# Where a two-layer attention kernel sums its softmax rows and runs its convolution: row sums of DMAs added on VectorE, the convolution's steps ended one tile earlier, reciprocals and position halves asked for later

## The chip, the cores and the metric

The kernel runs on one core of a Trainium2 chip. The metric is the device time of one execution in microseconds (us), lower is better. The engines of the core are TensorE (PE; its weight loads are listed as PEld), VectorE (DVE), ScalarE (ACT), GpSimd (POOL) and SyncE (SP, which here only issues DMAs). Each has its own queue of instructions; they meet through semaphores.

## The reference

Input x has the shape 2 x 256 x 64 x 64, float32. Two residual layers follow each other, each on a group-normalised x:

```python
x = x + _L0_conv_ref(_gn(x), qkv_w, qkv_b, 8)
x = x + _L1_conv_ref(_gn(x), ...)
```

Layer 0 is softmax attention with 8 heads of 32 channels over all 64 x 64 = 4096 pixels:

```python
attn_logits = jnp.einsum('bhci,bhcj->bhij', q, k) * scale
attn_weights = jax.nn.softmax(attn_logits, axis=-1)
out = jnp.einsum('bhij,bhcj->bhci', attn_weights, v)
```

Layer 1 adds two branches. In one, q, k, v (1x1 convolutions, with a position term made from pixel coordinates) go through attention among 64 pixels that lie 8 apart, and then, after more 1x1 convolutions, through attention within 8 x 8 blocks. In the other, a 1x1 mix of q, k and v over heads goes into a grouped 3 x 3 convolution. The kernel folds the latter's weights into one 3 x 3 convolution of the normalised x, 256 to 256 channels.

## The kernel before

**Stages.** The two images (batches b = 0, 1) are worked one after the other. Each goes through: loading x in 8 tiles `xts[t]` of 8 image rows (512 pixels) and its statistics; normalising and the projections q, k, v of layer 0; attention of layer 0 (`attention0`); layer 1's first attention (`layer1_first`); and its second one with the convolution (`layer1_second`, 8 tiles t). The `x` tiles stay in place: each stage adds its result into them. The x of batch 1 is loaded into the places of batch 0's x tiles when these come free. `Stats` (L256 to L271) makes the mean and 1/deviation, with two small matmuls `pm_l` (L261) and `pv_l` (L269) in between; batch 1's first projection matmul is `p_wk` (L333).

**attention0.** A group g is one head h = g // 2 and one half p = g % 2 of the queries (2048 of them, in four units u of 512). There are 16 groups, each with 32 steps j over 128 keys. For each step and unit, PE makes scores (L426: one 128 x 512 matmul), ScalarE the exponentials (L432), and PE multiplies them by v into `av` (L442, `quarters`: four column quarters of 32, one per unit, in the same PSUM bank). Scores lie in three PSUM tiles `sa`, `sb`, `sc` of 3, 2 and 2 banks. The exponentials go into a ring of 28 units, 7 steps; by their place in it the profile calls them `es` or `v`. Their order on PE, ScalarE and VectorE is the order in which the code is written; a scheduler orders the other queues, POOL and SP among them.

**Row sums.** The softmax denominators need the exponentials summed over all keys. VectorE sums most steps into `added` (the profile calls it `e`; two tiles of 128 x 2 x 512; L471 to L479). The steps listed in `SUMMED` (L380, seven of them) are instead summed by DMAs that POOL issues into four accumulators `acc` of 128 x 512 (L481 to L489; they lie in `es`, in `v` and, two of them, in one tile `pair`; the first of the seven copies, the rest accumulate). What is left is the sum over the 128 partitions: `sum_rows` (L502) multiplies `acc` and `added` by a matrix of ones, into the third bank of an `sa` tile. It is asked for at step 1 of the next group (`wanted`), and PE does it between two steps. `waiting` only asserts the order: the first copy into `acc` may come only after `sum_rows` of the group before.

**finish(g)** (L509) takes each group on: `rows` copied by ScalarE (L515), sent through DRAM to spread it over the partitions (`dense`), at step 8 reduced and inverted by VectorE (L521 to L523), sent back as `drec` and broadcast by four DMAs into `avs` (L524 to L526); at step 13 VectorE multiplies the group's `av` by it (L530) and SP writes the result to `ctx` (L532). The last group (15) goes through `finish_last` instead, without DMAs. `add_output` brings the results back and adds them into x, in two steps each, planned by `in_two` (L582 to L591).

**Position halves.** For layer 1, coordinates and their weights are split into a rounded part and the rest: `split` (L148) copies on ScalarE (L152) and subtracts on VectorE (L153). `stack` and `stack_positions` call it and then issue SP DMAs. These run in groups 1 to 5 of batch 0, in two calls: a beginning at step 3 or 15 and a rest at step 12 or 24, by the list `later`.

**layer1_second.** Per tile t: the branch q (two 1x1 convolutions, `phq`, `prq`), a convolution step, the branch k (`phk`, `prk`), scores `sp` (L890), softmax on VectorE and ScalarE, a convolution step, transposes `at` (L910), copies into `bd` (L919), values `pvs` (L873), the product `pc` (L928), and ScalarE's `res` (L939). Convolution has 16 steps per batch: 4 strips s of two tiles by 4 column terms q. Each has a transform on POOL (L785 to L802, one step ahead), 32 matmuls into `mm` (L811), one ScalarE copy and VectorE passes that add it into x tiles 2s and 2s+1 (L817 to L838). Tile 0 runs three steps, tiles 1 to 6 two, tile 7 one. When both x tiles of a strip have their four terms, VectorE adds `res` and x (L1132) and SP writes the output (L1135). `group_attention` takes `apart=True`: the first half of the values comes before the scores, the second after the `bd` copies, and both are copied by ScalarE.

Of the kernel before, what the change touches and what calls it, by code (L numbers as in the profile page):

```python
# [17 lines left out]
P = 128  # L18
# [22 lines left out]
def direct_layers(ctx: ExitStack, tc: tile.TileContext, a: dict, out: bass.AP, bad: bass.AP):  # L41
# [79 lines left out]
    def load_layer1():  # L121
        for name in ("fq2", "fk2"):
            wts[name] = load_const("wt_" + name, [P, KC, C], a[name].rearrange("(k p) m -> p k m", p=P))
        wts["b3"] = load_const("b3", [P, KC], a["b3"].rearrange("(k p) -> p k", p=P))
        wts["rate1"] = load_const("rate1", [P, 1], a["rate1"].partition_broadcast(P))
        wts["rate2"] = load_const("rate2", [P, 1], a["rate2"].partition_broadcast(P))


        posk, posq = w4([4, C], "posk"), w4([4, C], "posq")
        nc.gpsimd.dma_start(out=posk, in_=a["posk"])  # L130
        nc.gpsimd.dma_start(out=posq, in_=a["posq"])
        rows = const.tile([4, 1], F32, name="pos_rows")
        nc.gpsimd.memset(rows, 8.0)
        nc.gpsimd.memset(rows[0:1, :], 1.0)
        nc.vector.tensor_scalar(posq, posq, rows, None, ALU.mult)
        def stack(name, rows):
            wts[name] = const.tile([16, C], F32R, name="st_" + name)
            pair = split(rows, name)
            for g in range(4):
                nc.sync.dma_start(out=wts[name][4 * g : 4 * g + 4].bitcast(F32), in_=pair[:, g % 2, :].bitcast(F32))  # L140

        later.append(lambda: (lambda: stack("posq", posq)))
        later.append(lambda: (lambda: stack("posk", posk)))
# [3 lines left out]

    def split(rows, nm):  # L148

        n, cols = rows.shape  # L150
        pair = w4([n, 2, cols], f"pair_{nm}", F32R)
        nc.scalar.copy(pair[:, 0, :], rows)  # L152
        nc.vector.tensor_sub(pair[:, 1, :], rows, pair[:, 0, :].bitcast(F32))  # L153
        return pair


    kept_w = {name: dram.tile([P, KC, C], F32, name="kept_" + name) for name in ("w3", "fv")}
# [12 lines left out]
    def stack_positions(t):  # L170
        n = slice(t * T, (t + 1) * T)
        loc = w4([4, T], f"loc_{t}")
        nc.sync.dma_start(out=loc, in_=a["loc"][:, n])

        def rest():
            pair = split(loc, f"loc_{t}")
            for d in range(2):
                nc.sync.dma_start(out=loc_kept[:, d, :, n].rearrange("l r n -> r l n"), in_=pair.bitcast(F32))

        return rest  # L180

    def fold_products():

# [193 lines left out]

    RING, RING_A = 28, 17

    SUMMED = (5, 9, 13, 17, 21, 25, 28)  # L380


    SUMMED_LAST = (NJ - 2, NJ - 1)
# [1 line left out]
    def attention0(b, xts, held):  # L385
# [52 lines left out]
        def quarters(dst, lhs, rhs, start, stop, part=None):  # L438

            n = slice(0, T) if part is None else slice(part * T // 2, (part + 1) * T // 2)  # L440
            for u in range(4):
                nc.tensor.matmul(dst[HD0 * u : HD0 * u + HD0, n], lhs, rhs(u)[:, n], start=start, stop=stop)  # L442
# [57 lines left out]
                )  # L500

        def sum_rows(g, rows):  # L502
            waiting.clear()
            quarters(rows, ones, lambda u: acc[u], True, False)
            for j in SUMMED_LAST if g == last else ():
                quarters(rows, ones, lambda u: unit(g, j, u), False, False)
            quarters(rows, ones, lambda u: added[g][u // 2][:, u % 2, :], False, True)

        def finish(g):  # L509

# [68 lines left out]
        def at_block(g, j, what):  # L579
            also.setdefault((g, j), []).append(what)  # L580
# [7 lines left out]
        for w in (2, 3):  # L588
            in_two((last, 4), (last, 18), add_output(1, w, P - HD0))
        for w in (0, 1):  # L590
            in_two((last, 17), (last, 22), add_output(1, w))  # L591
        st = Stats(xts, f"l1_{b}")
        for t in range(NT):
            at_block(last - 2, 3 * t + 6, lambda t=t: st.tile(0, t))
# [5 lines left out]
        rests = {}  # L600
        for n, begin in enumerate(later):
            at_block(1 + n // 2, 3 + 12 * (n % 2), lambda n=n, begin=begin: rests.update({n: begin()}))
            at_block(1 + n // 2, 12 + 12 * (n % 2), lambda n=n: rests.pop(n)())
        later.clear()

# [3 lines left out]
        def steps():  # L609

            for done in range(NH0 * 2 * NJ):
                g, j = divmod(done, NJ)
                for _ in work_of(g, j):
                    yield done
                if g and j == 1:
                    wanted.append(late[0].send)
                    waiting.append(g)
                if g and j in (8, 13):
                    next(late[0])
                for what in also.get((g, j), ()):  # L620
                    what()
                if j == 4 and g % 2 == 0 and g // 2 + 1 < NH0:
                    fetch_head(b, g // 2 + 1, held)
                if j == NJ - 1:
                    avs = w4([P, 2, T], f"avs_{b}_{g}")
                    nc.scalar.copy(avs[:, 0, :], sums[g])
                    copied[g] = avs
                    late[:] = [finish(g)]
                    next(late[0])
                    if g + 2 < NH0 * 2:  # L630
                        fetch_queries(b, g + 2, held)
                yield done + 1
# [411 lines left out]
    def layer1_second(b, xts, feats, mean, rstd, shift, pacc):  # L1044
# [28 lines left out]
        for t in range(NT):  # L1073
            nt = f"sr_{b}_{t}"
            f = [
                feats[k][:, 8 * t : 8 * t + 8].rearrange("p o d e -> p (o d e)") for k in range(KC)
            ]

            def branch(one, two, col1, col2, nm):
                hid = w4([P, KC, T], f"h{nm}_{nt}")  # L1080
                for m in range(KC):
                    ph = bank([P, T], f"ph{nm}_{nt}_{m}")
                    for k in range(KC):
                        nc.tensor.matmul(  # L1084
                            ph, wts[one][:, k, m * P : (m + 1) * P], f[k], start=k == 0, stop=k == KC - 1
                        )
                    bn_relu(hid[:, m, :], ph, col1, m)
                res = w4([P, KC, T], f"r{nm}_{nt}")
                pr = [bank([P, T], f"pr{nm}_{nt}_{m}") for m in range(KC)]
                for k in range(KC):  # L1090
                    for m in range(KC):
                        nc.tensor.matmul(  # L1092
                            pr[m], wts[two][:, k, m * P : (m + 1) * P], hid[:, k, :], start=k == 0, stop=k == KC - 1
                        )
                for m in range(KC):
                    bn_relu(res[:, m, :], pr[m], col2, m)
                return res

            with tc.manual_schedule(engines={mybir.EngineType.PE}):
                q = branch("fq1", "fq2", V_FQ1, V_FQ2, "q")  # L1100
                for tt in {0: (3, 4)}.get(t, (t + 4,)):
                    if tt < NT:
                        to_image(tt)
                if t == 0:
                    wf = fetch_conv_weights(b)
                if t + 1 < NT:
                    conv()
                k = branch("fk1", "fk2", V_FK1, V_FK2, "k")
                res = w4([P, KC, T], f"res_{nt}")

                def to_res(m, pc, res=res):

                    bn_relu(
                        res[:, m, :].rearrange("p (d o e) -> p o d e", d=8, o=8),
                        pc.rearrange("p (o d e) -> p o d e", o=8, d=8), V_SRW, m,
                    )

                parts = group_attention(
                    nt, q, k, lambda c, w, f=f: f[c][:, w * P : (w + 1) * P], wts["fv"], to_res, apart=True
                )  # L1120
                next(parts)
                conv()
                next(parts)
                next(parts, None)
                if t == 0:
                    conv()
            conv_edges(xts, t)
            results[t] = res
            for n in sorted(n for n in results if done >= 4 * (n // 2 + 1)):
                res = results.pop(n)  # L1130
                for m in range(KC):
                    nc.vector.scalar_tensor_tensor(  # L1132
                        res[:, m, :], res[:, m, :], wts["rate1"], xts[n][:, m, :], ALU.mult, ALU.add
                    )
                nc.sync.dma_start(  # L1135
                    out=out[b, :, n * T : (n + 1) * T].rearrange("(k p) n -> p k n", p=P), in_=res
                )


    for b in range(B):  # L1140
# [15 lines left out]
        with tc.tile_pool(name=f"ps1_{b}", bufs=8, space=PSUM) as psum["ps"]:  # L1156
            between = layer1_first(b, xts, check, st)
        with (
            tc.tile_pool(name=f"ps2_{b}", bufs=4, space=PSUM) as psum["ps"],
            tc.tile_pool(name=f"pacc_{b}", bufs=1, space=PSUM) as pacc,  # L1160
        ):
            layer1_second(b, xts, *between, pacc)

# [557 lines left out]
```

## Time and profile before

| | us |
|---|---|
| three runs | 3258.98, 3260.95, 3265.7 (median 3260.95) |
| profiled run, its span | 3260.86, 3259.0 |

Where the time of the profiled execution goes, by stage (windows of the trace; busy us of each engine):

| stage | from to, us | length | PE | DVE | ACT | POOL |
|---|---|---|---|---|---|---|
| attention of layer 0, b = 0 | 108 to 1171 | 1063 | 1048.8 | 912.3 | 976.6 | 286.0 |
| layer 1 first, b = 0 | 1171 to 1350 | 179 | 152.6 | 149.2 | 73.1 | 9.5 |
| layer 1 second, b = 0 | 1350 to 1655 | 305 | 286.9 | 144.3 | 99.5 | 119.1 |
| loading, projection, b = 1 | 1655 to 1743 | 88 | 85.6 | 36.2 | 26.6 | 0.0 |
| attention of layer 0, b = 1 | 1743 to 2798 | 1055 | 1044.6 | 907.2 | 971.9 | 285.9 |
| layer 1 first, b = 1 | 2798 to 2969 | 171 | 146.8 | 62.0 | 59.6 | 0.8 |
| layer 1 second, b = 1 | 2969 to 3259 | 290 | 278.1 | 134.7 | 91.9 | 115.2 |

Read a row so: where an engine's busy time comes close to the length, little can be hidden behind something else there. Two thirds of the span are layer 0's attention. Busy time does not tell which wait ends last; for that the lists of waits and the timelines are needed. In those, a line names the engine, the source line, the operation, and the tiles as out<-in; in brackets stands the time for which the engine had been idle, and who ended it.

### The profile page before, as it was taken

The page shows a single profiled execution, that of the slowest core. Times are in us where ns is not written, and L with a number is a line of the kernel's source. Part 1 is how long each engine was busy: PE and PEld are TensorE (multiplying, and loading weights), DVE is VectorE, ACT ScalarE, POOL GpSimd, SP SyncE. Part 2 cuts the span into 40 slices and gives each one's busy share as a digit, 9 for nine tenths or more (in the row PEclk, how much of TensorE's full clock was granted, in tenths as well). Part 3 has the DMA queues.
Part 4 walks back from the last instruction along what each step waited for, and adds up shares of the span by engine and source line. Part 5 has one row for each costly group of instructions (what it writes and reads, how often), then busy time and mean ns, then how long its engine had stood idle before and what let it go on. Part 6 is the DMA issues. An engine that isn't in the chain of part 4 may idle for free. (4 is left out here: it accounts for less than half of the span.)

```text
span 3259.0 us, 62523 instructions
## 1 busy us (share of the span) xinstructions
PE 3129.8 (96%) x25113; PEld 1845.7 (57%) x25113; DVE 2394.0 (73%) x3122; ACT 2327.3 (71%) x2370; POOL 837.0 (26%) x929
## 2 busy tenths in 40 slices
PE   7999999999999979999989999999999999799998
PEld 4455555555555535676654555555555555356665
DVE  4688878987989898654446888879889798624443
ACT  2798989999999963523326999999999999624232
POOL 2122222222222220343201222322222222104431
PEclk9999999999999989999989999999999999899999
DMA  7967869679795641300149688796797956400000
GB/s 257 255 135 160 160 135 183 134 163 179 146 186 124 137 108 49 137 26 26 43 177 262 132 163 162 148 182 134 159 181 146 179 124 137 122 2 10 14 20 21
DMA packets 243916, 425.23 MB, mean 130 GB/s; under 512 B 99008, under 2 KB 109592, under 8 KB 241184
## 3 DMA queue, kind: packets, MB, share of 16 engines
q0 software_dynamic: 98336, 241.20, 38.3%
q1 hardware_dynamic: 145280, 179.93, 20.7%
q8 instruction: 199, 3.26, 0.4%
q14 instruction: 101, 0.83, 0.1%
HBM read 118.26 MB, written 67.86 MB: 57 GB/s over the span
## 5 line engine op out<-in xcount | busy, mean ns | idle before, releaser
L479 DVE TENSOR_TENSOR e<-e,es 128x1024 f32<-128x1024 f32 (+1 forms) x950 | 1035.4, 1151 | 59.4 <-ACT es L432 58.8
L442 PE MATMUL av<-es,v 128*32 128x256 f32 (+1 forms) x9644 | 746.9, 390 | 0.0
L432 ACT ACTIVATE es<-sa 128x1536 f32<-128x1536 f32 (+1 forms) x444 | 635.9, 1432 | 92.2 <-PE sa L426 46.5
L479 DVE TENSOR_TENSOR e<-e,v 128x1024 f32<-128x1024 f32 (+1 forms) x630 | 669.7, 1120 | 22.1 <-ACT v L432 21.7
L426 PE MATMUL sa<-q,k 128*128 128x512 f32 x1736 | 561.2, 430 | 14.0 <-issue 4.5
L442 PE MATMUL av<-v 128*32 128x256 f32 (+1 forms) x6228 | 506.9, 389 | 0.0
L442 PEld LDWEIGHTS av<-es,v 128*32 128x32 f32 x9644 | 316.5, 109 | 300.1 <-issue 161.3
L426 PEld LDWEIGHTS sa<-q,k 128*128 128x128 f32 x1736 | 280.2, 188 | 297.6 <-issue 139.9
L426 PE MATMUL sc<-q,k 128*128 128x512 f32 x1180 | 373.3, 397 | 10.2 <-ACT es L432 7.5
L426 PE MATMUL sb<-q,k 128*128 128x512 f32 x1180 | 371.4, 396 | 4.4 <-ACT es L432 2.3
L442 PEld LDWEIGHTS av<-v 128*32 128x32 f32 x6228 | 216.3, 109 | 178.4 <-issue 81.4
L432 ACT ACTIVATE es<-sc 128x1024 f32<-128x1024 f32 x296 | 306.4, 1035 | 7.0 <-DVE e L479 7.0
L432 ACT ACTIVATE v<-sc 128x1024 f32<-128x1024 f32 x294 | 304.4, 1035 | 0.9 <-DMA es<-v 0.7
L432 ACT ACTIVATE es<-sb 128x1024 f32<-128x1024 f32 x296 | 302.1, 1021 | 3.6 <-DMA acc<-es 3.6
L432 ACT ACTIVATE v<-sb 128x1024 f32<-128x1024 f32 x294 | 300.1, 1021 | 4.7 <-DVE e L479 3.0
L426 PEld LDWEIGHTS sc<-q,k 128*128 128x128 f32 x1180 | 209.2, 188 | 86.3 <-ACT es L432 20.5
L426 PEld LDWEIGHTS sb<-q,k 128*128 128x128 f32 x1180 | 220.1, 188 | 61.5 <-ACT es L432 4.9
L489 POOL DMA_DIRECT2D es<-es x118 | 101.5, 860 | 526.5 <-ACT es L432 469.8
L432 ACT ACTIVATE v<-sa 128x1536 f32<-128x1536 f32 (+1 forms) x146 | 209.2, 1433 | 34.0 <-PE sa L426 15.1
L811 PE MATMUL mm<-v,wf 128*128 128x256 f32 x1024 | 227.9, 381 | 0.0
L801 POOL TENSOR_TENSOR v<-col 128x512 f32<-128x512 f32 x128 | 161.8, 1294 | 228.5 <-PE sp_sr L890 93.3
L811 PEld LDWEIGHTS mm<-v,wf 128*128 128x128 f32 x1024 | 193.2, 190 | 33.1 <-issue 7.2
(240 smaller groups left out, 3319.4 us busy)
## 6 DMA issues: line engine op xcount, KB each, us to landing
acc<-es POOLq DMA_DIRECT2D x122, 512.0 KB, 6.2
acc<-v POOLq DMA_DIRECT2D x76, 512.0 KB, 6.3
es<-es POOLq DMA_DIRECT2D x136, 256.0 KB, 3.7
v<-es POOLq DMA_DIRECT2D x132, 256.0 KB, 4.6
k<-wk_halves SPq DMA_DIRECT2D x64, 512.0 KB
q<-wq_halves SPq DMA_DIRECT2D x256, 128.0 KB
v<-v POOLq DMA_DIRECT2D x92, 256.0 KB, 4.9
es<-v POOLq DMA_DIRECT2D x88, 256.0 KB, 3.8
```

The source lines that it names most:

```text
L426: nc.tensor.matmul(sc[:, i, :], held["k", g // 2][:, j * P : (j + 1) * P], held["q", g, u // 2][:, u % 2, :], start=True, stop=True,)
L432: nc.scalar.activation(dst, sc[:, i : i + m, :], AF.Exp, scale=SC0)
L442: nc.tensor.matmul(dst[HD0 * u : HD0 * u + HD0, n], lhs, rhs(u)[:, n], start=start, stop=stop)
L479: nc.vector.tensor_add(dst[:, s, :], dst[:, s, :], src)
L489: nc.gpsimd.dma_start(out=dst, in_=src, accum_op=ALU.add)
L801: (nc.gpsimd.tensor_add if plus else nc.gpsimd.tensor_sub)(dst, rows(one), rows(two))
L811: nc.tensor.matmul(mm[:, m, r, :], wf[:, k, 4 * r + q, m * P : (m + 1) * P], v[r // 2][:, r % 2, k, :], start=k == 0, stop=k == KC - 1,)
```

## The change

It has these parts:

1. In groups 0 to 14, `sum_rows` multiplies only `added` by ones. Before it, at step 0 of the next group, VectorE adds the four `acc` into `added` (two adds of 128 x 512 and one of 128 x 1024). `waiting` is moved accordingly. Group 15 is as before.
2. `SUMMED` names other steps, seven again.
3. `finish`'s reciprocal and multiply move from steps 8 and 13 to 9 and 17; `add_output(1, w)` for w = 0, 1 from steps 17 and 22 of the last group to 21 and 26.
4. The position halves are done in three calls instead of two: ScalarE's copy moves from step 12 (24) to step 8 (20), the subtraction and the DMAs stay.
5. Tile 7 of `layer1_second` runs no convolution step, tile 1 runs three. In tile 7 `apart` is false: scores first, then both halves of the values, the second copied by VectorE.
6. The pool of `mm` is opened ahead of the pool of the other PSUM tiles.

```diff
@@ -135,9 +135,16 @@
         nc.vector.tensor_scalar(posq, posq, rows, None, ALU.mult)
         def stack(name, rows):
             wts[name] = const.tile([16, C], F32R, name="st_" + name)
-            pair = split(rows, name)
-            for g in range(4):
-                nc.sync.dma_start(out=wts[name][4 * g : 4 * g + 4].bitcast(F32), in_=pair[:, g % 2, :].bitcast(F32))
+            pair, second = split(rows, name)
+
+            def rest():
+                second()
+                for g in range(4):
+                    nc.sync.dma_start(
+                        out=wts[name][4 * g : 4 * g + 4].bitcast(F32), in_=pair[:, g % 2, :].bitcast(F32)
+                    )
+
+            return rest
 
         later.append(lambda: (lambda: stack("posq", posq)))
         later.append(lambda: (lambda: stack("posk", posk)))
@@ -146,12 +153,12 @@
     later = []
 
     def split(rows, nm):
+
 
         n, cols = rows.shape
         pair = w4([n, 2, cols], f"pair_{nm}", F32R)
         nc.scalar.copy(pair[:, 0, :], rows)
-        nc.vector.tensor_sub(pair[:, 1, :], rows, pair[:, 0, :].bitcast(F32))
-        return pair
+        return pair, lambda: nc.vector.tensor_sub(pair[:, 1, :], rows, pair[:, 0, :].bitcast(F32))
 
 
     kept_w = {name: dram.tile([P, KC, C], F32, name="kept_" + name) for name in ("w3", "fv")}
@@ -172,12 +179,17 @@
         loc = w4([4, T], f"loc_{t}")
         nc.sync.dma_start(out=loc, in_=a["loc"][:, n])
 
-        def rest():
-            pair = split(loc, f"loc_{t}")
-            for d in range(2):
-                nc.sync.dma_start(out=loc_kept[:, d, :, n].rearrange("l r n -> r l n"), in_=pair.bitcast(F32))
-
-        return rest
+        def halves_of():
+            pair, second = split(loc, f"loc_{t}")
+
+            def rest():
+                second()
+                for d in range(2):
+                    nc.sync.dma_start(out=loc_kept[:, d, :, n].rearrange("l r n -> r l n"), in_=pair.bitcast(F32))
+
+            return rest
+
+        return halves_of
 
     def fold_products():
 
@@ -377,7 +389,7 @@
 
     RING, RING_A = 28, 17
 
-    SUMMED = (5, 9, 13, 17, 21, 25, 28)
+    SUMMED = (3, 7, 11, 15, 18, 22, 26)
 
 
     SUMMED_LAST = (NJ - 2, NJ - 1)
@@ -500,11 +512,11 @@
                 )
 
         def sum_rows(g, rows):
-            waiting.clear()
-            quarters(rows, ones, lambda u: acc[u], True, False)
-            for j in SUMMED_LAST if g == last else ():
-                quarters(rows, ones, lambda u: unit(g, j, u), False, False)
-            quarters(rows, ones, lambda u: added[g][u // 2][:, u % 2, :], False, True)
+            if g == last:
+                quarters(rows, ones, lambda u: acc[u], True, False)
+                for j in SUMMED_LAST:
+                    quarters(rows, ones, lambda u: unit(g, j, u), False, False)
+            quarters(rows, ones, lambda u: added[g][u // 2][:, u % 2, :], g < last, True)
 
         def finish(g):
 
@@ -588,7 +600,7 @@
         for w in (2, 3):
             in_two((last, 4), (last, 18), add_output(1, w, P - HD0))
         for w in (0, 1):
-            in_two((last, 17), (last, 22), add_output(1, w))
+            in_two((last, 21), (last, 26), add_output(1, w))
         st = Stats(xts, f"l1_{b}")
         for t in range(NT):
             at_block(last - 2, 3 * t + 6, lambda t=t: st.tile(0, t))
@@ -600,6 +612,7 @@
         rests = {}
         for n, begin in enumerate(later):
             at_block(1 + n // 2, 3 + 12 * (n % 2), lambda n=n, begin=begin: rests.update({n: begin()}))
+            at_block(1 + n // 2, 8 + 12 * (n % 2), lambda n=n: rests.update({n: rests[n]()}))
             at_block(1 + n // 2, 12 + 12 * (n % 2), lambda n=n: rests.pop(n)())
         later.clear()
 
@@ -612,16 +625,23 @@
                 g, j = divmod(done, NJ)
                 for _ in work_of(g, j):
                     yield done
+                if g and j == 0:
+
+                    for w in range(2):
+                        dst = added[g - 1][w]
+                        for s in range(2) if w == 0 else (slice(0, 2),):
+                            nc.vector.tensor_add(dst[:, s, :], dst[:, s, :], acc[s] if w == 0 else pair)
+                    waiting.clear()
                 if g and j == 1:
                     wanted.append(late[0].send)
-                    waiting.append(g)
-                if g and j in (8, 13):
+                if g and j in (9, 17):
                     next(late[0])
                 for what in also.get((g, j), ()):
                     what()
                 if j == 4 and g % 2 == 0 and g // 2 + 1 < NH0:
                     fetch_head(b, g // 2 + 1, held)
                 if j == NJ - 1:
+                    waiting.append(g)
                     avs = w4([P, 2, T], f"avs_{b}_{g}")
                     nc.scalar.copy(avs[:, 0, :], sums[g])
                     copied[g] = avs
@@ -1116,13 +1136,14 @@
                     )
 
                 parts = group_attention(
-                    nt, q, k, lambda c, w, f=f: f[c][:, w * P : (w + 1) * P], wts["fv"], to_res, apart=True
+                    nt, q, k, lambda c, w, f=f: f[c][:, w * P : (w + 1) * P], wts["fv"], to_res, apart=t + 1 < NT
                 )
                 next(parts)
-                conv()
+                if t + 1 < NT:
+                    conv()
                 next(parts)
                 next(parts, None)
-                if t == 0:
+                if t < 2:
                     conv()
             conv_edges(xts, t)
             results[t] = res
@@ -1156,8 +1177,8 @@
         with tc.tile_pool(name=f"ps1_{b}", bufs=8, space=PSUM) as psum["ps"]:
             between = layer1_first(b, xts, check, st)
         with (
+            tc.tile_pool(name=f"pacc_{b}", bufs=1, space=PSUM) as pacc,
             tc.tile_pool(name=f"ps2_{b}", bufs=4, space=PSUM) as psum["ps"],
-            tc.tile_pool(name=f"pacc_{b}", bufs=1, space=PSUM) as pacc,
         ):
             layer1_second(b, xts, *between, pacc)
```

## The prediction

> **What bounds the kernel now.** I read the page's busy table first, then windows by stage, then the waits, and last the timelines of the four places that the edits touch.
>
> ```profile
> PE 3129.8 (96%) x25113; PEld 1845.7 (57%) x25113; DVE 2394.0 (73%) x3122; ACT 2327.3 (71%) x2370; POOL 837.0 (26%) x929
> 200.00:1150.00 950.00, 939.06 (x9139) 527.53 (x9141) 816.26 (x831) 872.79 (x831) 255.85 (x312) 1.00 0.78 155
> 1850.00:2800.00 950.00, 942.70 (x9219) 531.40 (x9215) 822.22 (x832) 875.51 (x828) 258.37 (x315) 1.00 0.78 157
> ```
>
> The busy table covers the span of 3259.0 us. The windows (stretch, length, then busy us of PE, PEld, DVE, ACT, POOL) hold most of layer 0's attention, once per batch. TensorE is busy 939 of 950 us there, and the granted clock is 1.00. The share alone would not prove a bound, so I looked at PE's idle time too: 11 and 7 us, in a few lumps. TensorE bounds both stretches, ScalarE follows at 92%, VectorE at 86%. A group of 32 steps lasts about 66 us. Hence a matmul taken out is worth its duration, and VectorE work put in is free as long as nobody waits for it.
>
> The waits view (engine, tile and line, whom it waited for: us, times, longest) tells who waits for VectorE's inputs:
>
> ```profile
> POOL es L487 <- PE sa L442: 520.0, 30, 19.9
> DVE avs L530 <- DMA avs<-drec: 148.1, 24, 12.4
> DVE e L479 <- ACT es L432: 58.8, 63, 3.8
> ```
>
> VectorE stands still for 148 us at L530 (the row sums' reciprocals, coming back by DMA) and 59 us for fresh exponentials.
>
> **What the Trainium skill says.** (1) "TensorE: Matmul & The Clock Gate", Part 3 (packing small matmuls): matmuls in different column tiles overlap, and matmuls start and end in order. The trace agrees: the quarters below start 0.01 us apart, so four cost what one does. (2) Same page, "Architectural detail": VectorE's queue is strictly first in, first out. The trace agrees: nothing behind L530 starts in its 11.30 us wait. (3) "VectorE: DVE Perf Modes", the tier table: a float32 tensor_tensor has no faster mode than 1x, 2293 ns for 2048 elements; estimate for 1024, half of it: 1.15 us. The trace's adds of 128x1024 take 1.218 us (median), those of 128x512 0.68 us; I use these. (4) "DMA: Bandwidth & Descriptors", rules: an accumulating DMA must not meet another access of the same bytes. That is why `acc` may be written again only after VectorE has read it.
>
> **The change, part by part.**
>
> *Row sums.* The timeline of one group's row sums before:
>
> ```profile
> 526.65 0.59 PE L442 MATMUL sa<-es,ones 128*32 128x512 f32 x1
> 526.66 0.59 PE L442 MATMUL sa<-v,ones 128*32 128x512 f32 x1
> 526.67 0.60 PE L442 MATMUL sa<-acc,ones 128*32 128x512 f32 x2
> 527.08 0.59 PE L442 MATMUL sa<-es,ones 128*32 128x512 f32 x1
> 527.09 0.59 PE L442 MATMUL sa<-v,ones 128*32 128x512 f32 x1
> 527.10 0.60 PE L442 MATMUL sa<-acc,ones 128*32 128x512 f32 x2
> 527.51 1.04 PE L442 MATMUL sa<-e,ones 128*32 128x512 f32 x8
> ```
>
> The matmuls on `acc` (each of the float32 operands makes two passes) fill 526.65 to 527.51, 0.86 us without idle time. They go in 15 of 16 groups, twice: 30 x 0.86 = **25.8 us off PE**, on the path.
>
> VectorE gets 2 x 0.68 + 1.22 = 2.58 us per group, 77 us in all, at step 0 of the next group. Before, it idles 9 to 10 us per group (148.1/30 = 4.9 at L530, (58.8 + 21.7)/30 = 2.7 for exponentials, the rest smaller), so its load goes from about 57 to 59.5 of 65 us. In the 30 groups it finished a group's adds 4.2 to 13.1 us before PE used `added`; less 2.58, PE still finds the sums ready with 1.6 us or more. The last accumulating DMA was issued 14.6 to 19.5 us before the row sums and lands in 6.2 us; its step now comes two earlier, 4 us, while VectorE reads `acc` about 3 to 5 us earlier than PE did, so the new wait (queued behind it: VectorE's adds of steps 1 and on) finds its data. POOL's first copy waits for VectorE's adds instead of PE; it waited 520/30 = 17 us per group before, and the ring place of the exponentials that it reads is needed seven steps later. New waits: 0; they can't gain anything, and I bound them by 0.5 us per group (+15). SUMMED keeps seven steps: 0.
>
> *Reciprocals later, position halves in three.* The timeline (start, us; in brackets the idle time before, and its releaser) shows how a wait of VectorE gets to PE:
>
> ```profile
> 420.83 0.69 DVE L530 TENSOR_TENSOR avs<-avs 128x512 f32<-128x512 f32 x1 [11.30 <-DMA avs<-drec]
> 422.77 1.02 ACT L432 ACTIVATE es<-sc 128x1024 f32<-128x1024 f32 x1 [5.18 <-DVE e L479]
> 423.85 1.22 PE L426 MATMUL sc<-q,k 128*128 128x512 f32 x2 [4.53 <-ACT es L432]
> 285.78 0.73 PE L426 MATMUL sc<-q,k 128*128 128x512 f32 x2 [1.55 <-ACT es L432]
> 2183.27 0.73 PE L426 MATMUL sb<-q,k 128*128 128x512 f32 x2 [1.60 <-ACT v L432]
> ```
>
> The multiply waits, the adds behind it do not free exponentials, ScalarE has no slot, PE no scores. Most of the 148 us never reach PE; these lumps do: 4.53 + 1.55 + 1.60 + 0.2 smaller = 7.9 us. From reciprocal to multiply now lie 8 steps of 2.05 us, 16.4, not 5 (10.2). Where VectorE waited, reciprocal to multiply took 8 to 19 us, in two groups of batch 0 18.7 and 22.8 with the loc_kept transfers ahead in SP's queue. Pushing the multiply back removes most of each wait: over all groups at most 35.8 us of 148 are left. The position halves no longer make VectorE wait for ScalarE's copy (22.2 us in 6 waits at L153). The output steps in the last group come four steps later, still before their use: 0. **-8 us**, between 0 (the lumps return elsewhere) and -9.
>
> *Convolution out of tile 7.* The third step in tile 1 costs there what it saves in tile 7, 6.9 us of matmul: net 0, its transform (POOL, idle 74%) and its one `mm` buffer being ready as they are in tile 0, where the third step starts without a gap. The gain is at the ends. PE at the change of batch before:
>
> ```profile
> 1636.86 2.23 PE L928 MATMUL pc_sr<-bd,vs_sr 128*128 128x128 f32 x16
> 1650.57 0.56 PE L261 MATMUL pm_l<-mv_l,group 128*128 128x2 f32 x2 [11.49 <-DVE mv_l L260]
> 1651.96 0.59 PE L269 MATMUL pv_l<-d_l,group 128*128 128x2 f32 x2 [0.84 <-DVE d_l L266]
> 1655.10 1.22 PE L333 MATMUL p_wk<-xn,wqk 128*128 128x512 f32 x1 [2.54 <-DVE xn L283]
> ```
>
> From 1639.09 to 1655.10 PE idles 16.0 us, all but the two small matmuls. The next batch's last x tile could be loaded only once VectorE had finished the output of tile 6 and 7 (convolution step 16 adds into both): SP issued it at 1644.15, statistics started 1648.64. After, x tiles 6 and 7 get their last convolution term in tile 6, the load of x_7 goes out during tile 7 (27 us long, the load about 4.5), and `pm_l` waits only for the banks that ScalarE reads at the end (0.9 us after `pc`); then the 4.6 us from `pm_l` to `p_wk` stay: about 5.5 us in place of 16.0, **-10.5**. Against it, in tile 7 no convolution matmuls cover the softmax. With scores first and both value halves after them (3.8 us, softmax 2.5 us), PE waits 0.95 us for ScalarE's `rk` and 1.4 us for the `bd` copies that VectorE does behind the value copy (0.69 + 0.42 + 0.43): +2.35. Net **-8.2** (bounds -10.5 and +2.4).
>
> The end of batch 1 has the same +2.35 up to `pc`, but the chain after it shrinks: from `pc` at 3247.86 VectorE ran until 3252.48 through z, edges and four output passes, with two transfers behind it and the end at 3259.0. After, ScalarE's 1.6 us, two output passes of 0.7 us and one transfer follow. I take **-1.5** (between +1 and -3).
>
> *Pool order.* It only moves PSUM banks; no row prices it. 0, within 1 us either way.
>
> Sum on the span: -25.8 - 8 - 8.2 - 1.5 = -43.5; I give 1 back for waits that a faster PE uncovers at ScalarE. 3259.0 - 42.5 = 3216.5. The profiled run took 3260.86, 1.9 above its span; the three runs had 3258.98 to 3265.7, median 3260.95. So **3218 us** in the runs' measure.
>
> **The rivals.**
> B, the lumps do not come back as time: PE idle stays or VectorE's longer list makes new lumps of the same size. For it: VectorE goes to 91%. Only rows, transition and end then count: 3261 - 35.5 = 3225.5, up to 3235 with 0.3 us more per group.
> C, the gap between batches stays (x_7, a pool's release or weights hold `pm_l`): 3218 + 10.5 = 3228.5. Against it: x_7's place is free a tile earlier by the order of instructions.
> D, slower: VectorE becomes the bound. If reading `acc` waits for the last accumulation, or the adds arrive late, PE stands before the row-sum matmuls in every group. It decides from 42.5/30 = 1.4 us stall per group; at 3 us, +90 - 42.5: 3308. Against it: 1.6 us of slack in the worst group, 5 to 10 in most, and idle time of 5 us per group left.
> E, it doesn't do what it says: the tile 1 step stalls PE for a buffer for as long as it saves. Twice 6.9 us: 3232.
>
> **How the numbers follow.** Main case 0.60 (3211 to 3226), B 0.20, C with E 0.09, larger gains than the lumps I counted 0.05 (3205), D 0.06, part of which ends within 0.2%. 0.2%, 6.5 us, is about what a measurement of this kernel can tell from no change. Faster 0.93, same 0.02, slower 0.05. The range, 3208 to 3236, leaves out D and the ends of the others.
>
> **What would show it.** Right: no `acc` matmuls on `ones` but in the last groups; 3 adds more per group and a group near 65 us; L530's wait below 36 us; no PE idle above 1 us within attention but at its start; `p_wk` of batch 1 5 to 6 us after the last `pc`. Wrong: PE waiting for VectorE at `sa<-e,ones`, VectorE waiting for `acc` transfers, `pm_l` still waiting for the statistics, PE gaps before `mm` in tile 1.

## The result and the profile after

The changed kernel takes 3227.03 us (median of four runs, 3224.2 to 3230.66) beside 3260.55 us for the kernel before (four runs, the three of the table above among them); the ratio is 0.9895, 95% interval 0.9878 to 0.9912. That is 33.5 us less, where 42.5 were forecast. The profiled execution has a span of 3227.1 us, 31.9 less than the one before. Line numbers from here on are those of the changed kernel: the exponentials are L444, the adds into `added` L491, the multiply L542, the new adds of `acc` L633.

The busy table, and the windows over layer 0's attention (first score to last score) of both kernels; first the changed kernel:

```profile
PE 3106.4 (96%) x24873; PEld 1843.5 (57%) x24873; DVE 2484.7 (77%) x3230; ACT 2323.5 (72%) x2368; POOL 822.5 (25%) x913
108.98:1152.25 1043.27, 1033.11 (x10036) 586.26 (x10036) 951.88 (x978) 974.25 (x927) 278.40 (x341) 1.00 0.80 161
1720.70:2765.20 1044.50, 1031.68 (x10036) 586.66 (x10036) 945.91 (x964) 970.60 (x917) 278.46 (x341) 1.00 0.80 160
```

then the kernel before:

```profile
108.46:1170.00 1061.54, 1047.83 (x10155) 588.74 (x10156) 910.91 (x925) 975.57 (x927) 285.97 (x349) 1.00 0.78 158
1743.00:2797.60 1054.60, 1044.23 (x10155) 588.28 (x10156) 906.80 (x911) 971.54 (x917) 285.54 (x349) 1.00 0.79 158
```

Attention gave 18.3 and 10.2 us, 28.5 of the 31.9. (In a line of windows stand the stretch, its length, the busy time of PE, PEld, DVE, ACT and POOL, then PE's granted clock, the busy share of the DMA engines and GB/s.) VectorE works some 40 us more in each, and PE is still busy 99% of the time. The timeline of PE at a group's row sums, after:

```profile
256.48 0.61 PE L454 MATMUL av<-v 128*32 128x256 f32 x8
256.92 1.04 PE L454 MATMUL sa<-e,ones 128*32 128x512 f32 x8
257.77 1.05 PE L454 MATMUL av<-v 128*32 128x256 f32 x16
```

The block is 0.86 us long where it was 1.72 (526.65 to 528.37 in the kernel before), and PE does not wait ahead of it. The waits view of the changed kernel:

```profile
DVE e L491 <- ACT es L444: 91.3, 134, 2.5
DVE e L491 <- ACT v L444: 52.0, 64, 3.5
DVE avs L542 <- DMA avs<-drec: 12.5, 7, 2.5
```

The wait at the multiply fell from 148.1 us to 12.5. VectorE now spends its idle time in many short waits for ScalarE, at most 3.5 us long: it is ahead of its work, not behind. The new adds (L633) wait for nothing, and nobody waits for them.

PE's idle time within attention, summed over the trace, group 0 apart from the other fifteen (two batches together):

| | attention, us (b = 0, b = 1) | idle in group 0 | idle in groups 1 to 15 |
|---|---|---|---|
| before | 1061.55, 1054.66 | 5.9 | 18.2 |
| after | 1043.26, 1044.47 | 11.9 | 11.1 |

The idle time that the forecast wanted to win back was won (7.1 us less in groups 1 to 15), but group 0 gave 6.0 of it away. This is one of two places that the forecast had at zero. The timelines of ScalarE, PE and POOL in group 0 of the changed kernel:

```profile
117.57 0.55 POOL L499 DMA_DIRECT2D v<-es  x1
133.24 1.02 ACT L444 ACTIVATE es<-sc 128x1024 f32<-128x1024 f32 x1 [4.01 <-DMA v<-es]
134.31 1.22 PE L438 MATMUL sc<-q,k 128*128 128x512 f32 x2 [3.82 <-ACT es L444]
```

One of the first copies into `acc` is issued at 117.57. The ring place that it reads is still not free at 129, so ScalarE, and PE behind it, stand. It lands only 15.5 us after its issue; the first copies of groups 1 to 15 land in 2.3 to 6.0 us. The windows there show what goes with it, and what else it costs:

```profile
120.00:130.00 10.00, 10.00 (x102) 5.89 (x101) 8.65 (x8) 8.79 (x8) 0.89 (x1) 1.00 1.01 213
130.00:134.30 4.30, 0.49 (x3) 0.06 (x1) 1.86 (x3) 1.02 (x1) 0.86 (x1) 0.77 0.96 216
134.30:150.00 15.70, 15.69 (x138) 8.51 (x139) 10.82 (x10) 12.81 (x12) 4.24 (x5) 0.84 1.17 229
```

The DMA engines are full at the start of attention (share about 1; SP sends keys and queries there). A full share alone makes no lump: in the kernel before it is 1.09 from 400 to 419 us, and PE has no idle time there. And after the lump PE's clock is 0.84, as a mean over 15.7 us, although it is busy all the time.

The second place is the convolution. PE's and VectorE's timeline in tile 2 of batch 0, changed kernel:

```profile
1431.86 0.69 DVE L268 BATCH_NORM_STATS2 stats_l<-x 128x6 f32<-128x512 f32 x1 [4.79 <-DMA x<-in_x_dram]
1432.47 0.67 DVE L837 TENSOR_TENSOR z<-z,mm 128x512 f32<-128x512 f32 x1
1436.35 8.77 PE L831 MATMUL mm<-v,wf 128*128 128x256 f32 x32 [2.47 <-DVE z L840]
```

PE waits 2.47 us before `mm`, for VectorE's passes over the step before (that of the extra step in tile 1). Those were queued behind statistics of batch 1's x, which waited 4.79 us for their load. Batch 1, with no next batch, has no such gap. The six traces with this order of convolution steps (the changed kernel, e1, e5, e6, e8, e9) all have it in batch 0: 2.47 us in three, 3.69 us in e1, e5 and e6.

The change of batch went as forecast:

```profile
1626.18 2.02 PE L948 MATMUL pc_sr<-bd,vs_sr 128*128 128x128 f32 x16 [1.42 <-DVE bd L939]
1629.07 0.38 PE L273 MATMUL pm_l<-mv_l,group 128*128 128x2 f32 x2 [0.87 <-ACT res_sr L959]
1630.63 0.47 PE L281 MATMUL pv_l<-d_l,group 128*128 128x2 f32 x2 [1.18 <-DVE d_l L278]
1633.65 1.22 PE L345 MATMUL p_wk<-xn,wqk 128*128 128x512 f32 x1 [2.54 <-DVE xn L295]
```

`pc` ends at 1628.20, `p_wk` starts 5.45 us later. `pm_l` no longer waits for the statistics but for ScalarE.

### The profile page after: what moved, and what is told of

Its sections match the earlier page's. It is cut to its first block, busy times and chain, and to the rows that moved or that the text cites. A ratio compares the mean times of both kernels' runs of the same rounds, so it can differ in the third digit from the quotient of the medians.

```text
span 3227.1 us, 62236 instructions
## 1 busy us (share of the span) xinstructions
PE 3106.4 (96%) x24873; PEld 1843.5 (57%) x24873; DVE 2484.7 (77%) x3230; ACT 2323.5 (72%) x2368; POOL 822.5 (25%) x913
## 5 line engine op out<-in xcount | busy, mean ns | idle before, releaser
L491 DVE TENSOR_TENSOR e<-e,es 128x1024 f32<-128x1024 f32 (+1 forms) x956 | 1040.6, 1146 | 92.6 <-ACT es L444 91.3
L491 DVE TENSOR_TENSOR e<-e,v 128x1024 f32<-128x1024 f32 (+1 forms) x640 | 676.5, 1111 | 53.2 <-ACT v L444 52.0
L444 ACT ACTIVATE es<-sa 128x1536 f32<-128x1536 f32 (+1 forms) x444 | 635.6, 1432 | 94.6 <-PE sa L438 52.2
L438 PE MATMUL sa<-q,k 128*128 128x512 f32 x1736 | 561.9, 431 | 16.2 <-ACT es L444 5.5
L444 ACT ACTIVATE es<-sc 128x1024 f32<-128x1024 f32 x296 | 306.9, 1037 | 7.1 <-DMA v<-es 7.1
L444 ACT ACTIVATE es<-sb 128x1024 f32<-128x1024 f32 x296 | 302.1, 1020 | 5.0 <-DMA acc<-es 5.0
L444 ACT ACTIVATE v<-sc 128x1024 f32<-128x1024 f32 x294 | 304.9, 1037 | 0.2 <-DMA acc<-v 0.2
L444 ACT ACTIVATE v<-sb 128x1024 f32<-128x1024 f32 x294 | 300.0, 1020 | 0.4 <-DMA acc<-v 0.4
L444 ACT ACTIVATE v<-sa 128x1536 f32<-128x1536 f32 (+1 forms) x146 | 209.2, 1433 | 33.4 <-PE sa L438 13.7
```

Of the source, the lines that this page charges most:

```text
L438: nc.tensor.matmul(sc[:, i, :], held["k", g // 2][:, j * P : (j + 1) * P], held["q", g, u // 2][:, u % 2, :], start=True, stop=True,)
L444: nc.scalar.activation(dst, sc[:, i : i + m, :], AF.Exp, scale=SC0)
L491: nc.vector.tensor_add(dst[:, s, :], dst[:, s, :], src)
```

## The experiments

Theory S: the DMA-summed steps that come earlier, costed at nothing, put group 0's first copies into the full DMA queues. Theory T: the extra step in tile 1 meets the statistics on VectorE's queue. Against them stand L (the lumps were only shifted, or VectorE's longer list makes them), U (in tile 6 the extra step would only move the loss to the change of batch) and, for the whole change, the rivals B and D of the prediction. Each kernel was timed beside the kernel before; its median moved between 3259.6 and 3261.8 us from one set of runs to the next.

**Group 0 later (e1).** From the changed kernel:

```diff
+    SUMMED_FIRST = (5, 9, 13, 17, 20, 23, 26)
+    def summed(g):
+        return SUMMED_FIRST if g == 0 else SUMMED
...
-                if j in SUMMED:
+                if j in summed(g):
...
```

> The changed kernel, but group 0 of each batch keeps DMA-summed steps that begin at 5 (5, 9, 13, 17, 20, 23, 26), all other groups as changed. Theory S (the earlier steps put the first copies into the busy DMA stretch at the start of attention, so ring places come free late): PE's idle time in group 0 falls from 5.2 and 6.7 us to about 2.8 and 3.1 as before the change, 6 us in all; about 3221 us. Rival L (the lumps moved there from the later groups, or VectorE's longer list makes them): group 0 stays at 5 to 7 us, time stays at 3227.

Measured 3221.65 us, ratio 0.9872 (0.9853 to 0.9892). Group 0 idles 2.7 and 2.9 us, attention takes 1039.24 and 1040.54 us: 8.0 less than in the changed kernel, 6.3 of it idle time in group 0. The first copies still take 10.7 to 12.8 us to land, but they go out 3.2 us later after the first score, and their places are needed two steps later. S holds, L falls.

**Only group 0 earlier (e2).** The same function in the kernel before, with (3, 7, 11, 15, 18, 22, 26) for group 0 alone.

> The kernel before, with only group 0's DMA-summed steps at the changed places (3, 7, 11, 15, 18, 22, 26). Theory S: PE's idle time in group 0 rises from 2.8 and 3.1 us to 5 to 7 each, about 6 us slower than before, 3266. Rival L: no change, 3260.

Measured 3269.56 us, ratio 1.0024 (1.0013 to 1.0034): slower by this alone. Group 0 idles 5.7 and 5.5 us. S holds from the other side, without any of VectorE's new adds.

**The extra step in tile 6 (e3).** From the changed kernel:

```diff
-                if t < 2:
+                if t in (0, NT - 2):
                     conv()
```

> The changed kernel with the extra convolution step at the end of tile 6 instead of tile 1. Theory T (the 2.47 us gap before mm in tile 2 of batch 0 comes from VectorE's queue: the statistics of the next batch's x tile wait for its load ahead of the step's passes, and the next step follows too soon): no gap of PE before mm above 0.5 us, and the gap from the last pc to p_wk stays near 5.5 us: 2.5 us less, about 3224.5. Rival U: the passes of the last step run into tile 7, x_7 is loaded later and the gap to p_wk grows by more than 2.5 us: 3227 or more.

Measured 3225.37 us, ratio 0.9886 (0.9868 to 0.9904). The time alone hardly tells it from 3227.0, the trace does: the gap is gone from `mm`, and `p_wk` follows the last `pc` after 5.56 us. PE and VectorE in the same place of this kernel:

```profile
1426.21 7.07 PE L831 MATMUL mm<-v,wf 128*128 128x256 f32 x32
1427.34 1.29 DVE L268 BATCH_NORM_STATS2 stats_l<-x 128x6 f32<-128x512 f32 x2 [4.86 <-DMA x<-in_x_dram]
```

The statistics wait as before, but no unfinished convolution step stands behind them. The same 32 matmuls take 7.07 us where they took 8.77 after the gap, and the stretch between the two attentions is 562.96 us long, not 568.46. That stretch varies: it is 566.2 to 571.9 us long in the six traces with the extra step in tile 1, longest where the gap is 3.69 us, and 563.0 to 566.4 in the four with it in tile 6 (e3, e4, e10, e11), none of which has the gap. The means differ by 4.6 us. T holds, U falls.

**Both repairs (e4).**

> Both edits of the two kernels above together. If S and T hold: 6 + 2.5 us less than the changed kernel, about 3218.5. If L and U hold: 3227 or more.

Measured 3216.04 us, ratio 0.9854 (0.9837 to 0.9872). With the two terms repaired that the forecast had at zero, the time is 2 us from the forecast of 3218. That it comes so close is in part luck, as the last part on the prediction shows: two of its other terms are wrong in opposite directions.

**Row sums on PE again (e5).** From the changed kernel: `sum_rows` and `SUMMED` as before, the adds at step 0 out, the rest of the change kept.

```diff
-            if g == last:
-                quarters(rows, ones, lambda u: acc[u], True, False)
+            waiting.clear()
+            quarters(rows, ones, lambda u: acc[u], True, False)
...
-                            nc.vector.tensor_add(dst[:, s, :], dst[:, s, :], acc[s] if w == 0 else pair)
```

> The changed kernel with the row sums as before it: PE multiplies acc by ones in every group, VectorE adds nothing at step 0, and the DMA-summed steps are the old ones (5 to 28). Sum of my prediction: 25.8 us more PE work, less the 6 us that group 0's earlier steps cost: about 3247. Rival (VectorE's extra 77 us cost PE time by new waits): less than 15 us more than the changed kernel, below 3242.

Measured 3243.2 us, ratio 0.9951 (0.9933 to 0.9969); attention 1050.79 and 1049.37 us. Beside the changed kernel that is 16.2 us more, close to the rival's limit of 15, but the old `SUMMED` also takes away what group 0 had lost. The kernel to compare it with is e1, which begins at the same step in group 0: 20.4 us between the two attentions, 21.5 us between the medians. The row-sum matmuls are worth that, together with what the other steps of `SUMMED` do in groups 1 to 15, which was not tried alone. The block itself is 0.859 us shorter in the trace, in each of 30 groups, 25.8 us in all; some 5 us are lost again. Idle gaps account for 2.1 of them (16.5 us in e1, 14.4 here), and 1.7 are lost in e1 while PE is busy: after a lump of 1.66 us its clock is 0.83, as a mean over 10 us (1756.66 to 1766.66), and in e5 it shows no such drop within attention. The rest, some 1.6 us, was not pinned down.

The kernel before and e5 have the same PE work and steps of DMA sums in attention. Their difference there, 16.0 us, is what the later reciprocals gave, with the position halves and the output steps of the last group, while the row sums were on PE.

**Reciprocals at the old steps (e6).** From the changed kernel:

```diff
-                if g and j in (9, 17):
+                if g and j in (8, 13):
```

> The changed kernel with reciprocal and multiply at steps 8 and 13 again. As predicted for the lumps: VectorE's wait at the multiply rises from 12.5 us to 100 to 150 us and PE's idle time outside group 0 from 11.1 to 18 or more: 3234 or a little above. Rival (the lumps went for another reason, the order of VectorE's adds or the faster steps): PE's idle time outside group 0 stays within 2 us, 3227.

Measured 3240.01 us, ratio 0.9934 (0.9913 to 0.9956): 13 us more for two constants. Its four runs lie between 3232.72 and 3242.53 us, and the traced one is the slowest. The wait at the multiply is back:

```profile
DVE avs L542 <- DMA avs<-drec: 93.3, 17, 9.3
```

PE idles 16.2 us in groups 1 to 15, where the changed kernel has 11.1. The direction and the mechanism are as expected. The wait and the idle time are smaller than expected (100 to 150 us, 18 us or more), the time is longer. Between the two traces the attentions differ by 10.4 us; 3.3 us lie in the stretch between them, which the edit does not touch (the gap before `mm` is 3.69 us here). So some 10 us belong to the two constants, as far as one trace of each can tell. In one of the 30 groups the last new add ends at 1043.99 us here, 0.9 us after PE has begun that group's row sums; in the others the sums are ready 0.4 us or more ahead, where the changed kernel has 6.2 us at least. So without the later multiply VectorE's new adds have no room left in the worst group.

**Convolution as before (e7).** From the changed kernel, the tile loop of the kernel before.

```diff
-  apart=t + 1 < NT
+  apart=True
...
-                if t + 1 < NT:
-                    conv()
+                conv()
...
-                if t < 2:
+                if t == 0:
```

> The changed kernel with the convolution as before: one step in tile 7, two in tile 1, values apart in tile 7. From the parts measured in the trace: the gap to p_wk 16.0 in place of 5.45 us (+10.5), the gap before mm gone (-2.5), tile 7's two waits gone (-1.9 per batch), the end of batch 1 longer (+3.0): about +7, 3234. Rival (the move is worth nothing because what it closes opens elsewhere): 3227.

Measured 3231.2 us, ratio 0.9913 (0.9895 to 0.9932). The gap from `pc` to `p_wk` is 15.76 us again and there is no gap before `mm`. 4 us more than the changed kernel where 7 were expected; at 0.2% that can't be told from 7. The stretch between the attentions is 573.97 us, 5.5 longer than in the changed kernel and 4.8 longer than the mean of the six traces with that order.

**VectorE's new adds twice (e8).** Each add of `acc` is done twice, so `acc` counts twice in these softmax denominators.

```diff
+                            for _ in range(2):
-                            nc.vector.tensor_add(dst[:, s, :], dst[:, s, :], acc[s] if w == 0 else pair)
+                                nc.vector.tensor_add(dst[:, s, :], dst[:, s, :], acc[s] if w == 0 else pair)
```

> The changed kernel with VectorE's three adds of acc done twice in every group 0 to 14, so acc is counted twice in these denominators: 2.58 us more per group, 77 us in all. Theory (VectorE still has room, about 4 us per group): PE's idle time in attention rises by less than 10 us, 3227 to 3237. Rival D (VectorE is at its limit): a part of the 77 us that matters, 3250 to 3300, with PE waiting for VectorE before the row sums.

Measured 3227.4 us, ratio 0.9907 (0.9888 to 0.9925): no difference. VectorE is busy 2555.1 us, 70 more, and PE's idle time in attention is 23.8 us, 0.8 more. The sums are ready 6.2 to 9.5 us before PE uses them in the changed kernel and 2.6 to 6.8 us here. What shrank is VectorE's waits for ScalarE's exponentials, in the waits view of this kernel:

```profile
DVE e L491 <- ACT es L444: 51.8, 84, 2.9
DVE e L491 <- ACT v L444: 26.5, 39, 3.7
```

Rival D falls with room to spare.

**Position halves and pools as before (e9).** Both undone in the changed kernel.

```diff
-            at_block(1 + n // 2, 8 + 12 * (n % 2), lambda n=n: rests.update({n: rests[n]()}))
-            at_block(1 + n // 2, 12 + 12 * (n % 2), lambda n=n: rests.pop(n)())
+            at_block(1 + n // 2, 12 + 12 * (n % 2), lambda n=n: rests.pop(n)()())
...
+            tc.tile_pool(name=f"ps2_{b}", bufs=4, space=PSUM) as psum["ps"],
             tc.tile_pool(name=f"pacc_{b}", bufs=1, space=PSUM) as pacc,
-            tc.tile_pool(name=f"ps2_{b}", bufs=4, space=PSUM) as psum["ps"],
```

> The changed kernel with the two edits undone that I costed at nothing or nearly so: position halves copied and subtracted in one call at step 12 (24), and the pool of mm opened second. Prediction's view: VectorE's wait for ScalarE at the halves comes back (up to 22 us in 6 waits, in groups 1 to 5 of batch 0), PE's idle time in those groups grows by 2 us at most: 3227 to 3229. Rival: one of the two carried part of the gain, 3233 or more.

Measured 3226.92 us, ratio 0.9889 (0.9865 to 0.9913): the same. VectorE's waits at the halves are back (22.6 us in 8 for the coordinates, 8.2 us in 2 for the weights), and PE's idle time in groups 1 to 5 of batch 0 is about 1 us in both kernels. With the multiply out of the way these waits reach nobody.

**Group 0 from step 7 (e10)**, with both repairs.

```diff
-    SUMMED_FIRST = (5, 9, 13, 17, 20, 23, 26)
+    SUMMED_FIRST = (7, 10, 13, 17, 20, 23, 26)
```

> The kernel with both repairs (group 0's DMA-summed steps later, the extra convolution step in tile 6), but group 0 begins at step 7 (7, 10, 13, 17, 20, 23, 26). If the DMA queues of the start of attention hold the ring places, a later first copy finds them emptier: idle time of group 0 below 3 us per batch, 3213 to 3216. If what is left there is the start itself: 3216, unchanged.

Measured 3212.87 us, ratio 0.9843 (0.9823 to 0.9864), group 0 idles 2.0 and 1.4 us. The later group 0 begins, the sooner its first copies land: 10.8 to 16.9 us from step 3 (changed kernel), 10.7 to 12.8 from step 5 (e1), 8.5 to 9.7 from step 7, with 11.9, 5.6 and 3.4 us of idle time. So part of what the kernel before lost in group 0 came from the same cause. Whether the time gains by it is not shown: beside e4 the intervals overlap, and e11, with the same group 0, has an attention 5.2 us longer in its trace, only 0.8 us below e4's.

**Values of tile 7 copied by ScalarE (e11)**, on top of e10.

```diff
-  wts["fv"], to_res, apart=t + 1 < NT
+  wts["fv"], to_res, True, apart=t + 1 < NT
```

> The kernel before this one, and in tile 7 ScalarE copies both halves of the values, so that VectorE's bd copies do not queue behind one. The wait of 1.42 us before the last pc of each batch falls to 0.7 us or less: 1 to 2 us less than the kernel before this one. Rival: ScalarE's copy comes as late as VectorE's did, no difference.

Measured 3213.23 us, ratio 0.9843 (0.9822 to 0.9863). The wait before the last `pc` falls from 1.49 to 1.04 us per batch, less than expected, and 0.9 us in all does not show in the time. e10 and e11 are the fastest kernels of the study, some 14 us below the changed one.

## Why the prediction was right, and where it was off

**Where the time lies.** 3227.0 us is within the range of 3208 to 3236, but just outside the main case (3211 to 3226) and among the figures of rival B (3225.5 to 3235). The time alone does not decide between them. The traces do: idle time in groups 1 to 15 fell by 7.1 us, and undoing the later multiply brings it back (e6), so B's mechanism falls. The sign "PE gaps before `mm`" that the prediction named for being wrong did show, in tile 2. Of the signs for being right one failed in a small way: outside its start, each attention keeps a lump of 1.28 us in its last group, as the kernel before has there (1.27).

**Right: the bound.** PE bounds attention. Work taken from it counts. A second 77 us of VectorE work beside it cost nothing that could be measured (e8), and the first 77 us cost at most the 5 us or so that are missing from the 25.8. The forecast put the room at 4 to 5 us per group with 1.6 us of slack in the worst one. The measured slack is 6.2 us at least, and in the worst group it is used up with the multiply at its old step (e6): taking the multiply's wait out of VectorE's queue gave back the room that the adds took.

**Right: the lumps, and how they arise.** Multiply, adds, exponentials, scores: e6 brings the wait and the lumps back with two constants. Mis-sized: the term "-8 us" measures 16.0 with the row sums on PE (kernel before against e5) and 10.4 with them on VectorE (e6 against the changed kernel). Idle time explains 9.7 of the 16.0. For part of the rest, look at the windows after the longest lump of the kernel before:

```profile
419.00:424.00 5.00, 0.47 (x3) 0.15 (x1) 3.17 (x4) 1.02 (x1) 0.00 (x0) 0.77 0.23 58
424.00:440.00 16.00, 16.00 (x134) 8.83 (x134) 16.00 (x17) 14.02 (x14) 5.62 (x7) 0.86 0.65 117
286.00:300.00 14.00, 13.83 (x139) 7.71 (x139) 14.00 (x14) 13.29 (x13) 5.38 (x7) 1.00 0.75 138
```

After 4.53 us of idle time PE ran at a clock of 0.86, as a mean over 16 us: another 2.2 us lost while it was busy. After 1.55 us (third line) it stayed at 1.00. I counted idle time alone; in the windows of 950 us that I had read, this drop vanishes and the clock shows as 1.00. Some 4 of the 16.0 us stay unexplained.

**Mis-sized: "25.8 us off PE".** 20.4 us arrive in attention (e5 against e1). The duration was right (0.859 us in 30 groups), the allowance of 1 us for new waits was too small.

**Wrong: "SUMMED keeps seven steps: 0".** The step looked at the number of DMAs and at who waits for the last of them, not at when the first is issued. In group 0 the first one goes out 2.7 us earlier (117.0 us, not 119.7), into full queues that free the place ScalarE needs no sooner (133.1 us, not 132.8). 8.0 us in attention (e1 against the changed kernel, e2 from the other side).

**Wrong: "The third step in tile 1 ... net 0".** I compared it with the third step of tile 0, which has no output, and so no next x tile, behind it. In tile 1 VectorE's order puts a wait for that tile's load ahead of the passes that free `mm`. 2.47 us of idle time and 1.7 us of slower matmuls, in batch 0 alone; 4.6 us as the mean over the traces with and without it.

**Right: the ends.** pc to `p_wk` 16.0 to 5.45 us (forecast 5.5), tile 7's price 0.52 + 1.42 = 1.94 us (forecast 2.35). At the end of batch 1, from the last `pc` to the end it is 11.1 us before and 8.4 after; with tile 7's 1.94 that is -0.8, where -1.5 was forecast. In the span it does not show: from the last score of batch 1 to the end it is 461 us before and after. Halves and pools: nothing (e9). Rival C falls, and of rival E's 14 us some 4 came true. No run here tests what the prediction says of accumulating DMAs that meet another access.

The errors partly cancel, which is luck: two zeros cost 8.0 and some 4 us, the rows gave 5 less, the lumps 8 more (taken in the order kernel before, e5, e1, changed kernel). That is about the 9 us by which the forecast missed; it is no closer an account than that, since the same code between the attentions takes up to 5.7 us more or less from one trace to the next. The two attentions together repeat within 2.4 us in three traces (the changed kernel, e3, e7) and within 0.2 in two (e1, e4), but differ by 5.2 in e10 and e11; sizes read from one trace each are no surer than that.

## What to carry to other kernels

A step that moves in time without changing in number need not be free: ask what its first instance meets where it now stands, the start of a stage above all, where loads fill the DMA queues. A wait at the head of an in-order queue holds up what stands behind it, so a value that comes back through DRAM should be used several steps after its request; here two constants were worth some 10 us. Such a move can pay for another: it is the later multiply that left the new adds room. Last, compare a step that is moved with one that has the same neighbours, not only the same work.

## What the runs showed of the hardware

An idle lump of TensorE can cost more than its length. In the kernel before, PE's clock is 0.50 for the 4.65 us after the lump of 4.53 us and 1.00 from there on; in the changed kernel it is 0.50 for 3.3 us (1436.35 to 1439.65) after the gap of 2.47 us, and the 32 matmuls there take 8.77 us in place of 7.07. The length of the lump alone does not decide it. The lines below begin at the end of a lump of 4.53 us (kernel before), 1.66 us (e1), 1.23 us (with 0.40 us more soon after it) and 1.65 us (both e6):

```profile
423.85:428.50 4.65, 4.65 (x28) 2.17 (x29) 4.65 (x6) 3.50 (x3) 2.60 (x3) 0.50 0.71 125
1756.66:1766.66 10.00, 10.00 (x78) 5.29 (x82) 6.17 (x6) 8.32 (x8) 4.52 (x6) 0.83 0.98 182
2172.50:2182.00 9.50, 9.09 (x71) 4.86 (x72) 9.50 (x10) 7.47 (x7) 2.63 (x3) 0.82 0.98 224
420.20:430.00 9.80, 9.80 (x99) 5.53 (x100) 9.80 (x9) 9.78 (x10) 2.79 (x4) 1.00 0.83 159
```

So the lump of 1.23 us was followed by a drop and that of 1.65 us was not. In the kernel before, the clock stayed at 1.00 after 1.55 us, and after 1.60 us with 0.41 more; in e2 it was 0.83 over the 10 us after 2.04 us. What else decides it, these runs do not show.
